# Layer 1's plan: Silu pieces a round later and pinned in ScalarE's order, the attention's exponentials a round later and beside the mixer's

## Chip, cores and metric

One core of a Trainium2 chip. The metric is the device time of one execution in microseconds, the median of the runs shown. In the text PE is TensorE, DVE VectorE, ACT ScalarE, POOL GpSimd, and SP the engine that issues most of the DMAs.

## The reference

A two-layer decoder over 32 sequences of 128 tokens of width 256 in fp32. Layer 0 is an attention with a latent, a cross attention and a mixture of experts (two of eight). Layer 1, which this change is about, has three blocks, each behind a layer norm and added to its input:

```python
x = x + _L1_attn_ref(_layernorm(x, axis=-1), ...)   # gated linear recurrence in chunks of 64, then an MLP with silu
x = x + _L1_xattn_ref(_layernorm(x, axis=-1), ctx_1024, ctx_1024, ...)   # one softmax over 128 keys per token
x = x + _L1_ffn_ref(_layernorm(x, axis=-1), ...)    # quantized linear, convolution of 3 taps, silu, quantized linear
```

In the first block `q` is normalized with a root mean square (here a logarithm and an exponential), the MLP takes `silu(h2 @ fc_w.T) @ proj_w.T`. The second takes `softmax(vis_key @ lang_key.T * scale)`. The third is

```python
h = bit_linear(x, w1)                       # activations rounded to 8 bits by the row's largest value
h = depthwise_conv1d(h.transpose(0, 2, 1), conv_w, conv_b)   # 3 taps along the tokens
h = jax.nn.silu(h.transpose(0, 2, 1))
return bit_linear(h, w2)                    # again rounded by the row's largest value
```

## The kernel before

Layer 0 runs first (attention, then the experts up to about 1150 us). Layer 1 then works in 16 units `u` of two sequences each (`U = 2`, so 256 tokens). A unit goes through four groups of pieces: `d_` (the recurrence), `m_` (the MLP), `e_` (the attention over the context) and `f_` (the quantized block with its convolution). Each piece is a small function in `unit(u)` that issues a few instructions.

The table `PLAN` gives each piece a round, and a new unit starts every `STEP = 11` rounds. So round `t` holds the pieces of several units, each at another stage: a software pipeline in which some seven units are under way at once. Within a round the pieces are issued in the order of the units, older ones first, and then in the plan's order. A scheduler orders the instructions of each engine from this program. `tc.keep_in_program_order(i)` pins instruction `i` behind all that was traced before it on its engine; TensorE's matmuls and transposes (helpers `mm`, L207, and `turned`, L210) and the DMAs of `fetch` are all pinned in this way. The engines run their own streams in order and wait for each other by semaphores.

The pieces that the text speaks of, in the order in which a unit meets them:

- `fetched` issues two DMAs of `yr` on SP (`fetch`, L719); `added` (L1163) adds them to `x` on VectorE, which begins the unit's way.
- `d_stats`, `d_nb`, `d_norm` (L1093), `d_scaled` (L1100), `d_flip` (copy L1112): statistics on VectorE, the root `rs_d` on GpSimd (L1082), `nb_d` on VectorE (L1088), two passes on ScalarE, transposes on TensorE and the copy `hT_d`. `d_q`, `d_a`, `d_k`, `d_g`, `d_v` are the products with `hT_d`. `al_d` (L1201, L1202) and the scans (L1239, L1245) are on VectorE.
- `d_q2` takes `Ln` on ScalarE (L1219), `d_rms` takes `Exp` (L1222) and multiplies on GpSimd (`qn_d`, L1223). `d_state` and `d_gate` follow on VectorE (L1248, L1252, L1254), with a subtraction on GpSimd (L1249) between.
- `m_fc` applies Silu on ScalarE to four products (`sT_m`, L1280). `m_stats` takes the statistics of `x1`, with `rs_m` on GpSimd, and adds `x1` to `x` there (L1269). `hn_m` is `m_scaled` (L1100).
- `e_stats` loads `kv_e` from DRAM on SP (L1298, two buffers, so that a load waits for the `lv_e` of the unit two before). `e_s` makes the scores, and their largest value `nm_e` (L1334). `e_exp` takes two exponentials of 128x128 on ScalarE (L1339), `e_soft` (L1345, L1347) normalizes them into `at_e`, `e_at` transposes them and makes `lv_e` (L1360); `vv_e` is L1321, and `x<-x,y_e` L1366.
- `f_h(k)`, for four pieces `k` of two hidden chunks: product and scaling `d_f` on VectorE (L1399). `f_z(k)`: the middle tap on ScalarE (L1404). `f_taps(k)`: a tap on VectorE for each of the two chunks (L1414), one on ScalarE (`e_f`, L1418, two buffers), and their sum on GpSimd (L1420). `f_silu(k)`: Silu in place on ScalarE (L1427). `f_top(k)`: the largest value over half of the chunks on VectorE (L1433, joined in L1438). `f_am`, `f_rows` (copy `rows2`, L1147) and `f_round(k)` (L1454, L1455) quantize. `f_out` adds the last product to `x` (L1468, `x<-o_f`) and stores it.

ScalarE keeps one table of functions at a time; where the next function is not in it, the built program has a table load (ACT_TABLE_LOAD, under the line of the function that needs it).

Of the kernel before, what the change touches and what calls it, by code (L numbers as in the profile page):

```python
# [13 lines left out]
AF = mybir.ActivationFunctionType  # L14
# [62 lines left out]
def decoder(ctx: ExitStack, tc: tile.TileContext, a: dict, out: bass.AP):  # L77
    nc = tc.nc
    V, A, PE, GP = nc.vector, nc.scalar, nc.tensor, nc.gpsimd
# [919 lines left out]
    def ternary(wf, ones, asum):  # L999
# [19 lines left out]
        (13, "d_v d_q2"), (14, "d_rms d_scan2"), (15, "d_state"), (16, "d_gate"), (18, "m_y"),  # L1019
        (19, "m_stats"), (20, "m_scaled"), (22, "m_flip"), (26, "m_fc0 m_fc1"), (27, "m_fc2 m_fc3"),  # L1020
        (29, "m_out0"), (30, "m_out1 m_out2"), (31, "m_out3"), (32, "e_stats"), (33, "e_nb"),
        (34, "e_norm"), (36, "e_flip"), (39, "e_k e_v"), (45, "e_s"), (47, "e_exp"), (48, "e_soft"),
        (50, "e_at"), (53, "e_y"), (54, "f_stats"), (55, "f_norm"), (56, "f_quant"), (58, "f_flip"),
        (60, "f_h0"), (62, "f_z0 f_h1"), (63, "f_z1 f_h2"), (64, "f_taps0 f_taps1 f_h3"),
        (65, "f_silu0 f_silu1"), (66, "f_z2"), (67, "f_top0 f_z3"), (68, "f_taps2"), (70, "f_silu2"),
        (71, "f_taps3"), (72, "f_silu3"), (73, "f_top1"), (75, "f_am"), (78, "f_rows"),
        (79, "f_round0 f_round1 f_round2"), (81, "f_round3"), (89, "f_out"),
    )

# [5 lines left out]
    def layer1(wd):  # L1035
# [8 lines left out]
        with (  # L1044
# [12 lines left out]
            def sb(tag, name, bufs=1, dt=F32, shape=(2, T)):  # L1057
                of = late if tag in ("z", "d", "kv", "s", "zi") else pool
                return of.tile([P, *shape], dt, tag=tag, name=name, bufs=bufs)
# [7 lines left out]
            def sm(tag, name, w=U, bufs=3):  # L1067
                return small.tile([P, w], F32, tag=f"l_{tag}", name=f"{tag}_{name}", bufs=bufs)
# [81 lines left out]
            def unit(u):  # L1150
# [185 lines left out]
                def e_exp():  # L1336
                    o["at"], o["den"] = sb("at", f"at_{e_}", 2, shape=(U, S)), sm("den", e_)
                    for i in range(U):
                        A.activation(  # L1339
                            o["at"][:, i, :], o["s"][:, i, :], AF.Exp, bias=o["nm"][:, i : i + 1],  # L1340
                            accum_out=o["den"][:, i : i + 1],
                        )

                def e_soft():
                    V.reciprocal(o["den"], o["den"])  # L1345
                    for i in range(U):
                        V.tensor_scalar(o["at"][:, i, :], o["at"][:, i, :], o["den"][:, i : i + 1], None, ALU.mult)  # L1347
# [76 lines left out]

                def f_silu(k):
                    z = o["z"][:, 2 * k : 2 * k + 2, :]
                    A.activation(z, z, AF.Silu)  # L1427

                def f_top(k):

# [43 lines left out]
                for k in range(4):  # L1474
                    for of in (m_fc, m_out, f_h, f_z, f_taps, f_silu, f_top, f_round):
                        pieces[f"{of.__name__}{k}"] = partial(of, k)
# [9 lines left out]
            for u in range(CTX0, NU):  # L1486
                made = context(u, wcs, lambda n: sb("d", n, 4), lambda n: sb("kv", n, 2, shape=(2, U * D)))
                for what, r in zip(("load", "keys", "values"), CTX_ROUNDS[u - CTX0]):
                    between.setdefault(r, []).append(made[what])
            units = [unit(u) for u in range(NU)]  # L1490
            pieces = {r: names.split() for r, names in PLAN}
            for t in range(STEP * (NU - 1) + PLAN[-1][0] + 1):
# [94 lines left out]
def program(arrays):  # L1587
    import concourse.bacc as bacc

    nc = bacc.Bacc("TRN2", target_bir_lowering=False, num_devices=1)  # L1590
    args = {
        k: nc.dram_tensor(f"in_{k}", v.shape, mybir.dt.from_np(v.dtype), kind="ExternalInput").ap()
        for k, v in arrays.items()
    }
    out = nc.dram_tensor("out", arrays["x"].shape, F32, kind="ExternalOutput").ap()
    with tile.TileContext(nc) as tc:
        decoder(tc, args, out)
    return nc
# [9 lines left out]
```

## Time and profile before

| what | value |
|---|---|
| median of 3 runs | 1908.31 us (1905.58 to 1917.17) |
| the profiled execution, its own time | 1910.32 us |
| its span, first to last instruction | 1908.5 us |
| busy over the span: PE, DVE, ACT, POOL | 91%, 59%, 56%, 21% |
| from 1357 to 1685.5 us: PE, DVE, ACT, POOL | 301.25, 282.68, 237.37, 111.49 of 328.50 us |
| layer 1's table loads, each 1283 ns | L1339 29, L1219 16, L1280 16, L1222 3, L1427 3 |
| granted TensorE clock, mean | 0.949 |

Shares over the whole span mix stages with different limits: the experts keep VectorE and ScalarE mostly idle, layer 1 does not. The second row of busy times is eight units of layer 1's steady part, with all groups of pieces under way. In an answer on waits, a line reads "engine, what waited, <- whom it waited for: us in total, times, longest us". In a timeline a line reads "start, duration, engine, line, operation, out<-in, count, and in brackets the idle time just before and what ended it".

### The profile page before, as it was taken

Reading aid. Unit: us, or ns where it says so; the run is one execution under the profiler, and the core shown is the slowest. Engines: PE = TensorE matmul, PEld = TensorE weight load, DVE = VectorE, ACT = ScalarE, POOL = GpSimd, SP = SyncE. Lnnn points to the kernel's source line nnn. Section 1 sums busy time; section 2 is a strip of 40 time slices with the busy share of each in tenths; the row PEclk is TensorE's granted clock in tenths of the full one; section 3 lists DMA queues with packets and bytes.
Section 4 is the critical chain, followed back from the end, with each engine's and each line's share of the span. In section 5 each row is a group of like instructions: output and inputs, shape, how many; then the busy total and the mean of one; then the engine's idle time right before and its main releaser. Section 6 shows DMA issues by size and latency. Waiting matters only on the chain.

```text
span 1908.5 us, 33114 instructions
## 1 busy us (share of the span) xinstructions
PE 1744.7 (91%) x12336; PEld 1427.5 (75%) x12336; DVE 1124.4 (59%) x3767; ACT 1069.7 (56%) x2380; POOL 410.2 (21%) x413
## 2 busy tenths in 40 slices
PE   6999998999888899999999999999899989999853
PEld 3777766776667688888888888788777778778742
DVE  6878775687775613111111104546788888888797
ACT  4565558788884532322232224556777677677662
POOL 4101000000000222222222212222333333333221
PEclk9999998899997799999999999999999999999975
DMA  6000010111001776666676644200000100010000
GB/s 199 2 2 2 13 35 23 34 54 37 24 13 45 254 301 207 243 226 207 216 247 211 215 139 169 72 23 23 23 28 28 50 28 29 29 34 18 28 16 18
DMA packets 58531, 170.12 MB, mean 89 GB/s; under 512 B 6272, under 2 KB 35328, under 8 KB 47616
## 3 DMA queue, kind: packets, MB, share of 16 engines
q1 hardware_dynamic: 51840, 150.14, 23.3%
q0 software_dynamic: 6528, 17.83, 2.4%
q8 instruction: 99, 1.62, 0.4%
q14 instruction: 64, 0.52, 0.1%
HBM read 142.26 MB, written 25.69 MB: 88 GB/s over the span
## 4 chain that ended last, share of the span: by engine, by line
PE 54%; DVE 27%; ACT 8%; POOL 4%; DMA 3%; issue 2%; SPq 0%; POOLq 0%; DVEq 0%; ACTq 0%
PE h L207 12%; PE y L207 12%; ACT sd_b L604 3%; DVE top_f L1433 3%; DMA yr<-ys 3%; DVE z_f L1414 2%; DVE sd_b L594 2%; PE st_a L207 2%; PE et_b L210 2%; PE y_a L207 2%; PE s_a L207 2%; PE od_a L207 2%; PE m_m L207 1%; PE s_b L207 1%; DVE z_f L1454 1%
## 5 line engine op out<-in xcount | busy, mean ns | idle before, releaser
L925 ACT ACTIVATE hTs<-h,moe 128x256 f32<-128x256 f32 (+1 forms) x320 | 140.9, 442 | 334.5 <-PE h L207 324.6
L207 PE MATMUL h<-xTs,moe 128*128 128x256 f32 (+1 forms) x1280 | 243.0, 348 | 1.0 <-DVE xTs L913 1.0
L207 PE MATMUL y<-moe,hTs 128*128 128x256 f32 x1088 | 241.5, 379 | 0.0
L207 PEld LDWEIGHTS h<-xTs,moe 128*128 128x128 f32 x1280 | 214.9, 191 | 24.8 <-DVE xTs L913 1.2
L207 PEld LDWEIGHTS y<-moe,hTs 128*128 128x128 f32 x1088 | 203.8, 190 | 26.0
L604 ACT ACTIVATE sd_b<-sd_b,nan_b 128x128 f32<-128x128 f32 x512 | 153.1, 390 | 29.5 <-DVE nan_b L601 29.5
L913 DVE COPY xTs<-xs 128x512 f32<-128x512 f32 (+1 forms) x40 | 24.4, 610 | 217.7 <-PE xs L210 217.7
L937 DVE TENSOR_TENSOR yt<-y,moe 128x256 f32<-128x256 f32 x68 | 28.8, 424 | 204.7 <-PE y L207 204.7
L594 DVE CUSTOM_DVE_ANT_0 sd_b<-nd_b,s_b 128x128 f32<-128x128 f32 x512 | 112.0, 281 | 21.4 <-PE s_b L207 19.0
L207 PE MATMUL m_m<-wd,sT_m 128*128 128x256 f32 x512 | 119.1, 381 | 0.0
L207 PE MATMUL f_m<-hT_m,wd 128*128 128x256 f32 x512 | 118.9, 388 | 0.0
L1420 POOL TENSOR_TENSOR z_f<-z_f,e_f 128x508 f32<-128x508 f32 x64 | 72.0, 1125 | 211.3 <-DVE z_f L1414 113.2
L938 POOL DMA_INDIRECT ys<-yt,whither x68 | 67.3, 990 | 190.1 <-DVE yt L937 181.9
L207 PEld LDWEIGHTS f_m<-hT_m,wd 128*128 128x128 f32 x512 | 97.7, 195 | 13.4 <-issue 0.5
L899 POOL DMA_INDIRECT xr<-xs,who x68 | 66.0, 970 | 188.8 <-PE xs L210 156.9
L207 PEld LDWEIGHTS m_m<-wd,sT_m 128*128 128x128 f32 x512 | 95.6, 191 | 12.5 <-ACT sT_m L1280 0.2
L145 POOL TENSOR_TENSOR rs_c<-ve_c,mhalf 128x4 f32<-128x4 f32 x8 | 8.1, 1011 | 414.7 <-DVE ve_b L143 286.7
L1427 ACT ACTIVATE z_f<-z_f 128x512 f32<-128x512 f32 x64 | 40.3, 630 | 87.0 <-POOL z_f L1420 86.9
L511 DVE TENSOR_REDUCE nm<-s_a 128x4 f32<-128x512 f32 x128 | 78.8, 676 | 5.1 <-PE s_a L207 4.9
L1404 ACT ACTIVATE z_f<-d_f,pv 128x256 f32<-128x256 f32 x128 | 69.8, 590 | 19.8 <-DVE d_f L1399 19.8
L207 PE MATMUL s_b<-kEO_b,qT_b 32*128 32x256 f32 x512 | 59.7, 453 | 21.1 <-ACT kEO_b L380 17.1
L541 ACT ACTIVATE et_a<-st_a 128x512 f32<-128x512 f32 x128 | 66.4, 613 | 19.0 <-PE st_a L207 19.0
(378 smaller groups left out, 3825.6 us busy)
## 6 DMA issues: line engine op xcount, KB each, us to landing
moe<-in_moe SPq DMA_DIRECT2D x40, 1156.0 KB, 5.9
moe<-in_moe SPq DMA_DIRECT2D x40, 1024.0 KB, 5.2
ckv<-kvc SPq DMA_DIRECT2D x16, 512.0 KB, 3.1
yr<-ys SPq DMA_DIRECT2D x32, 256.0 KB, 3.8
kv_e<-ckv SPq DMA_DIRECT2D x16, 512.0 KB, 3.3
x<-in_x SPq DMA_DIRECT2D x8, 512.0 KB, 9.1
cT_b<-in_ctxT SPq DMA_DIRECT2D x8, 512.0 KB, 3.8
xs<-xn_c SPq DMA_DIRECT2D x8, 512.0 KB, 2.9
```

The source lines that it names most:

```text
L207: tc.keep_in_program_order(PE.matmul(out, lhsT=lhsT, rhs=rhs, start=start, stop=stop))
L511: V.tensor_reduce(nms[i % 2][:, at : at + 2 * (P - HD)].rearrange("p (e x) -> p x e", e=2)[:, :2, :], sp[r], AX.X, ALU.max, negate=True,)
L541: A.activation(et[:, r].rearrange("p j q -> p (j q)"), st[r], AF.Exp)
L594: V.tensor_tensor_reduce(sd[:, r, j, :], nd[:, i, :], sp[r][:, j, :], SLOPES[head(r, j)], -3e38, ALU.add, ALU.max, mx[:, 4 * r + j : 4 * r ...
L604: A.activation(sd[:, r, j, :], sd[:, r, j, :], AF.Exp, bias=nan[:, 4 * r + j : 4 * r + j + 1])
L899: GP.indirect_dma_start(out=xr[h], out_offset=None, in_=xs[:, :], in_offset=bass.IndirectOffsetOnAxis(ap=who[:, q + h : q + h + 1], axis=0),)
L925: A.activation(hT[:, hc, : n * P], p, AF.Relu, bias=b1[:, hc : hc + 1])
L938: GP.indirect_dma_start(out=ys[:, :], out_offset=bass.IndirectOffsetOnAxis(ap=whither[:, q + h : q + h + 1], axis=0), in_=yt[:, h, :], in_ ...
L1404: A.activation(o["z"][:, hc, :], o["d", k][:, j, :], AF.Identity, scale=cw[:, hc, 1:2], bias=cb[:, hc : hc + 1],)
L1420: GP.tensor_tensor(z[:, :, : S - 1], z[:, :, : S - 1], e.rearrange("p h (b t) -> p (h b) t", b=U)[:, :, 1:], ALU.add,)
L1427: A.activation(z, z, AF.Silu)
L1433: V.tensor_reduce(o["top"][:, k, :], o["z"][:, 4 * k : 4 * k + 4, :].rearrange("p h t -> p t h"), AX.X, ALU.max, apply_absolute_value=True,)
```

## The change

The plan is altered in these places: `e_exp` goes from round 47 to 48 and `e_soft` from 48 to 49; `f_silu0` and `f_silu1` go from round 65 to 66, behind `f_z2`; `f_silu2` goes from 70 to 71, behind `f_taps3`; `f_silu3` goes from 72 to 73, `f_top1` from 73 to 74 and `f_am` from 75 to 76. Round 47 of a unit is also round 14 (`d_rms`) of the unit three behind it, which is traced later in that round. The exponentials of `e_exp` and the Silu of `f_silu` are pinned behind what was traced before them on ScalarE. Nothing else is altered. Lines after the edits are two to three further down in the changed kernel (L1404 is L1406 there, L1420 is L1422, L1433 is L1436, L1468 is L1471).

```diff
-        (34, "e_norm"), (36, "e_flip"), (39, "e_k e_v"), (45, "e_s"), (47, "e_exp"), (48, "e_soft"),
+        (34, "e_norm"), (36, "e_flip"), (39, "e_k e_v"), (45, "e_s"), (48, "e_exp"), (49, "e_soft"),
...
-        (65, "f_silu0 f_silu1"), (66, "f_z2"), (67, "f_top0 f_z3"), (68, "f_taps2"), (70, "f_silu2"),
-        (71, "f_taps3"), (72, "f_silu3"), (73, "f_top1"), (75, "f_am"), (78, "f_rows"),
+        (66, "f_z2 f_silu0 f_silu1"), (67, "f_top0 f_z3"), (68, "f_taps2"), (71, "f_taps3 f_silu2"),
+        (73, "f_silu3"), (74, "f_top1"), (76, "f_am"), (78, "f_rows"),
...
                     for i in range(U):
-                        A.activation(
+                        e = A.activation(
                             o["at"][:, i, :], o["s"][:, i, :], AF.Exp, bias=o["nm"][:, i : i + 1],
                             accum_out=o["den"][:, i : i + 1],
                         )
+
+                        tc.keep_in_program_order(e)
...
                     z = o["z"][:, 2 * k : 2 * k + 2, :]
-                    A.activation(z, z, AF.Silu)
+
+                    tc.keep_in_program_order(A.activation(z, z, AF.Silu))
```

## The prediction

> **What bounds the kernel now.** I read the page first, then the busy time by stage, then the waits, then one cycle in order of time. The edit touches only layer 1's plan, so only the part from about 1200 us counts. There one unit of two sequences enters per cycle. The `kv_e` loads start at 1356.90 and again, eight cycles later, at 1685.54: 328.64 / 8 = 41.08 us per cycle.
>
> ```profile
> ACT z_f L1427 <- POOL z_f L1420: 53.0, 32, 4.7
> 1357.00:1685.50 328.50, 301.25 (x1594) 255.38 (x1594) 282.68 (x727) 237.37 (x459) 111.49 (x105) 0.99 0.10 32
> ...
> DVE x L1163 <- DMA yr<-ys: 24.5, 8, 3.8
> DVE pre_d L1252 <- POOL pre_d L1249: 6.3, 8, 0.8
> DVE top_f L1433 <- ACT z_f L1427: 4.5, 7, 1.7
> DVE xn_f L1376 <- POOL rs_f L1082: 2.8, 8, 0.4
> DVE u_d L1244 <- POOL u_d L1213: 2.3, 2, 1.2
> DVE z_f L1414 <- ACT z_f L1404: 1.6, 8, 0.2
> DVE pre_d L1248 <- POOL qn_d L1223: 1.5, 1, 1.5
> ```
>
> These are the waits and the busy time of the eight cycles. The second line gives length, then busy PE, PEld, DVE, ACT, POOL: PE 92%, DVE 86%, ACT 72%. ScalarE's large wait, 53.0 us for GpSimd before the Silu, is idle time of the engine with most room, and so worth nothing by itself. VectorE's waits sum to 43.5 us, 5.4 per cycle; 24.5 of them are the fetch of `yr`, which the edit does not touch. The cycle closes like this:
>
> ```profile
> 1602.73 0.68 DVE L1360 TENSOR_TENSOR lv_e<-lv_e,kv_e 128x512 f32<-128x512 f32 x1
> ...
> 1607.50 0.88 DVE L1163 SCALAR_TENSOR_TENSOR x<-yr,rw,x 128x256 f32<-128x256 f32 x2 [2.85 <-DMA yr<-ys]
> ...
> 1626.37 1.09 POOL L1420 TENSOR_TENSOR z_f<-z_f,e_f 128x508 f32<-128x508 f32 x1 [2.14 <-DVE ms_d L1176]
> ...
> 1626.40 1.07 DVE L1177 TENSOR_TENSOR ms_d<-ms_d,mv_d 128x2 f32<-128x2 f32 x1
> ```
>
> `lv_e` frees the buffer that the `kv_e` load on SP's queue waits for, `yr` is queued behind that load, and VectorE stands at L1163 until it lands (4.1 to 4.4 us from the end of `lv_e`). Then VectorE runs nearly solid until the next `lv_e`. So a cycle is VectorE's work plus its waits, in its own order. The last row shows 0.16 us of work taking 1.07 while GpSimd adds `z_f`; the same happens to L1138 (0.98 us at 1831.22) and L1414 (1.23 at 1844.92), each beside such an add.
>
> ```profile
> 1614.55 0.63 ACT L1427 ACTIVATE z_f<-z_f 128x512 f32<-128x512 f32 x1 [1.20 <-POOL z_f L1420]
> 1615.21 0.51 ACT L1100 ACTIVATE hn_m<-x_m,rs_m 128x256 f32<-128x256 f32 x1
> 1615.63 0.57 ACT L1112 COPY hT_d<-pt_d 128x512 f32<-128x512 f32 x1
> ...
> 1616.24 2.00 PE L207 MATMUL q_d<-hT_d,wd 128*128 128x256 f32 x8 [1.46 <-ACT hT_d L1112]
> ...
> L1339 ACT ACT_TABLE_LOAD x29 | 37.2, 1283 | 0.5
> ```
>
> Here `hT_d` stands behind the Silu pieces on ScalarE, TensorE waits for it, and the attention's exponentials (L1339) cost 29 table loads, two in most units.
>
> **The change, part by part.** The built order of the changed kernel has the same instructions on PE, DVE, POOL and SP, and 13 table loads fewer on ACT (55 against 68): both exponentials now stand behind the mixer's `exp` (L1222) and share its load. TensorE's order within a cycle and SP's queue do not move; nothing is moved past a DMA. What moves is ACT's order, and with it DVE's and POOL's.
>
> *Loads.* 13 x 1.283 = 16.7 us of ACT, counted at nothing: ACT is idle 28% of the cycle, and DVE's waits for what these loads delay (L1248, for `qn_d`) are 1.5 us in eight cycles. Without that cover they would be worth the whole 16.7. The Trainium skill (ScalarE: Activation LUTs, "What ACT_TABLE_LOAD costs") counts a further drain with each switch, 2.66 us in all. The rows do not show it: the load of 1591.28 is followed by its function at 1592.57, 1.29 later. By the page ACT would be spared 34.6 us, still on an engine with room.
>
> I now walk one cycle. Zero is L1163 at 1607.50; the next is at 1648.66, 41.16 later. Durations are those of the same instructions in this cycle.
>
> *Silu behind other work.* The taps' first pass L1404 of piece 2 no longer waits behind Silu 1: it starts when `d_f` is there, 3.66 instead of 3.97. VectorE's taps of piece 2 gain nothing, since GpSimd's add L1269 runs until 4.64 beside them (they began at 1612.09, which is 4.59). `rs_m` follows at 6.2 to 6.9, then `hn_m` twice, `hT_d` at 7.8 instead of 8.1: TensorE gets `hT_d` 0.4 earlier, which nothing on VectorE waits for (`al_d` was ready at 13.1 and taken at 14.59).
>
> *Taps of piece 3.* In the new DVE order the first of them stands right behind `x<-x,y_e` (L1366), before the statistics; it used to come last, at 17.9. It needs ACT's pass of piece 3, which comes after `hT_d` and ends at 9.2. VectorE is free at 7.2: a new wait of 2.0. GpSimd's add of piece 2 starts at about 8.75 and runs 1.1, to 9.85; if it shuts the taps out as in the rows above, the wait is 2.65. Queued behind it: both statistics, `top_f`, `al_d` and the scan, so everything that closes the cycle.
>
> *`rs_d`.* The second statistics of `d` now come just before their use, and on POOL `rs_d` (0.70) is behind the add of piece 3 (1.09), which itself waits for the last taps. VectorE waits from the taps to `nb_d`: 0.09 + 1.10 + 0.70 + 0.03 less 0.17 of own work = 1.75, or about 2.1 if `ve_d` is shut out by that add. This used to be hidden behind the quantization.
>
> *`top_f` of half 1* (1.88) leaves this stretch together with its wait (0.47) and the shut-out of `ms_d` (0.90). From L1163 to `x<-o_f`: 22.53 before; after, 22.53 - 1.88 - 0.47 - 0.90 + 2.03 + 1.75 = 23.06, or with both shut-outs 24.03. So +0.53 to +1.50.
>
> *From `x<-o_f` to the end of `lv_e`:* 14.27 before. `top_f` comes here (+1.85), `rows2` is copied 0.2 late because ACT stands at `xn_d`, which waits for the late `nb_d`; the wait at L1252 goes (-0.87 with its issue) since `at_e` now lies between; `at_e` and the rounding lose some 0.25 less each to GpSimd. Sum 14.95: +0.68.
>
> A cycle is then longer by 1.2 to 2.2 us. I take 2.0, near the upper end, since three rows of the trace show the shut-out. Below these, a bound from the other side: if every VectorE wait but the fetch went, a cycle would shrink by (43.5 - 24.5) / 8 = 2.4.
>
> *Where it ends.* There are nine such cycles (eight, and one more before fetching stops): 9 x 2.0 = 18. Before 1357 TensorE is busy 93% and carries the same work in the same order: 0. In the drain there are two more cycles with the piece 3 wait but fewer stages to hold up: +1, bounds -2 to +5. Sum +19: 1910.3 us + 19 = 1929.3 for an execution like the profiled one (span 1908.5, 1.8 us around it). That execution lies 0.11% above the median of 1908.31, so on the median 1927.3. Its own range is 1916 to 1940.
>
> **The rivals.** *Faster.* ACT was what held the cycle, through the Silu pieces ahead of `hT_d`. For it: 15.2 us of TensorE waits for `hT_d` in eight cycles, and `hT_d` does come earlier. Against it: VectorE never waits for what `q_d` feeds. If it is so, and the new waits prove short, the 2.4 per cycle go: 9 x 2.4 = 21.4, 1887 on the median.
>
> *No net effect.* VectorE's work is the same, and the waits only change places: the moved `top_f` fills what `rs_d` opens, GpSimd's adds come a little later than in my walk. This ends within 3 us of 1908. It is also what follows if the edit does not act, which the built order speaks against.
>
> *Much slower.* `at_e` now stands behind `top_f` on VectorE and falls some 3 us later in the cycle. TensorE does not reach `at_e`'s transposes without it, and behind them in its order are `vv_e` and the product for `d_f` 1, which VectorE takes before L1163. In the walk they end 1.15 us before the fetch lands. If `at_e` is over 1.15 later still, each us beyond that costs 9: two us past it make 1945.
>
> **How the numbers follow.** A measurement of this kernel can tell about 1% from no change (19 us). I give the forecast 0.62: 0.42 of it above 1927.4 and 0.20 below, since its sum sits at that line. Faster 0.12; no effect 0.18; much slower 0.08. So slower by over 1%: 0.42 + 0.08 = 0.50; within: 0.20 + 0.18 = 0.38; faster: 0.12. The range runs from 1895, which cuts off most of the fast case, to 1942.
>
> **What would show it.** ACT table loads 68 to 55. In a cycle: VectorE idle 2 to 2.7 us at the taps of piece 3, put down to ACT's L1406 or hidden in a longer instruction; 1.7 to 2.1 at `nb_d` for POOL's `rs_d`; none at L1252; the `yr` wait near 3 as before; ACT's 53.0 us before the Silu mostly gone with no gain from it; the `kv_e` loads 43 us apart. The forecast is wrong if these loads come 41.1 apart or closer, or if TensorE at `at_e` rather than VectorE sets when L1163 is reached.

## The result, and the profile after

| | before | after |
|---|---|---|
| median, six runs each on one chip | 1908.54 us (1905.25 to 1917.17) | 1928.3 us (1925.4 to 1932.11) |
| ratio after / before, 95% interval | | 1.0109 [1.0083, 1.0135] |
| the profiled execution, its span | 1910.32, 1908.5 us | 1932.11, 1930.3 us |

The change makes the kernel 1.1% slower. To see where, I use one mark per unit, the start of `lv_e` on VectorE; there are 16. Between the third and the twelfth lie the nine cycles that the prediction counts. In the profiled executions:

| stretch | before | after | difference |
|---|---|---|---|
| layer 0 and the first unit, to the first `lv_e` | 1276.06 | 1274.03 | -2.0 |
| filling, first to third `lv_e` | 80.13 | 75.63 | -4.5 |
| nine cycles, third to twelfth | 369.49 (41.05 each) | 388.95 (43.22 each) | +19.5 |
| twelfth `lv_e` to the end | 182.82 | 191.69 | +8.9 |
| span | 1908.5 | 1930.3 | +21.8 |

The first row is no effect of the change: the first `lv_e` came at 1268.15 to 1281.00 in the 14 kernels profiled for this study, which share all of layer 0. A single profile is no better than that there. The span's 21.8 us also compare two single executions, the one after being the longest of its six; between the medians lie 19.8. The cycles are more even, but each kernel's come from one profile: single ones lie between 39.45 and 42.45 us before and between 41.99 and 44.22 after, so some tenths between two kernels can be scatter.

The first block below is the waits and busy times of the changed kernel over its nine cycles ("engine, what waited, <- whom for: us in all, times, longest"; the line of numbers is the window, its length, and busy PE, PEld, DVE, ACT, POOL).

```profile
1349.66:1738.61 388.95, 346.94 (x1801) 293.88 (x1800) 320.89 (x819) 252.59 (x505) 119.52 (x117) 0.97 0.09 31
...
DVE vv_e L1321 <- PE vv_e L207: 25.1, 9, 3.7
DVE nb_d L1088 <- POOL rs_d L1082: 14.1, 9, 1.6
DVE d_f L1401 <- PE h_f L207: 8.9, 9, 1.4
DVE z_f L1416 <- ACT z_f L1406: 5.9, 9, 1.4
DVE x L1163 <- DMA yr<-ys: 3.2, 4, 1.1
...
PE at_e L210 <- DVE at_e L1349: 30.3, 9, 5.4
...
ACT z_f L1406 <- DVE d_f L1401: 40.6, 18, 3.2
ACT xn_d L1093 <- DVE nb_d L1088: 31.5, 9, 3.9
```

VectorE is busy 35.65 us per cycle (320.89 / 9) against 35.43 before; its waits sum to 7.32 against 5.34. So of the 2.17 us by which a cycle grew, 1.98 are new VectorE waits. The list has also changed its members. The fetch of `yr`, 27.3 us in nine cycles before, is down to 3.2; in its place VectorE waits 25.1 for TensorE's `vv_e` and 8.9 for its `h_f`. TensorE waits 30.3 for `at_e` (4.4 before). ScalarE's wait before the Silu is out of its list, and so is TensorE's wait for `hT_d`. Two of these lines in the kernel before, over its nine cycles:

```profile
DVE x L1163 <- DMA yr<-ys: 27.3, 9, 3.8
...
PE at_e L210 <- DVE at_e L1347: 4.4, 6, 0.7
```

Of the table loads, these are left for the attention's and the mixer's exponentials (29 and 3 before):

```profile
L1222 ACT ACT_TABLE_LOAD x16 | 20.5, 1283 | 0.3
L1339 ACT ACT_TABLE_LOAD x3 | 3.8, 1283 | 0.1
```

One cycle of the changed kernel, VectorE in order of time, from one L1163 to the next. The bracket is the idle time before and what ended it:

```profile
1613.17 0.69 DVE L1321 TENSOR_TENSOR vv_e<-vv_e,rv 128x512 f32<-128x512 f32 x1 [3.72 <-PE vv_e L207]
...
1614.38 0.87 DVE L1163 SCALAR_TENSOR_TENSOR x<-yr,rw,x 128x256 f32<-128x256 f32 x2
...
1621.83 0.69 DVE L1401 TENSOR_TENSOR d_f<-h_f,rows_f_sb 128x512 f32<-128x512 f32 x1 [1.36 <-PE h_f L207]
1622.69 0.69 DVE L1368 TENSOR_TENSOR x<-x,y_e 128x512 f32<-128x512 f32 x1 [0.17 <-PE y_e L207]
1623.66 0.92 DVE L1416 SCALAR_TENSOR_TENSOR z_f<-d_f,pv,z_f 128x254 f32<-128x254 f32 x1 [0.28 <-ACT z_f L1406]
...
1637.25 0.16 DVE L1088 SCALAR_TENSOR_TENSOR nb_d<-mv_d,rs_d 128x2 f32<-128x2 f32 x1 [1.65 <-POOL rs_d L1082]
...
1637.79 0.87 DVE L1471 SCALAR_TENSOR_TENSOR x<-o_f,dq_f,x 128x256 f32<-128x256 f32 x2
...
1645.73 1.92 DVE L1436 TENSOR_REDUCE top_f<-z_f 128x256 f32<-128x1024 f32 x1
...
1649.30 1.04 DVE L1349 TENSOR_SCALAR at_e<-at_e,den_e 128x128 f32<-128x128 f32 x2
...
1652.37 0.68 DVE L1362 TENSOR_TENSOR lv_e<-lv_e,kv_e 128x512 f32<-128x512 f32 x1
```

L1163 at 1614.38 has no bracket: its data had long landed, and what held VectorE is `vv_e`. TensorE's side of that is one line:

```profile
1650.29 0.43 PE L210 MATMUL at_e<-cst,at_e 128*128 128x128 f32 x2 [3.12 <-DVE at_e L1349]
```

TensorE stood 3.12 us before `at_e`, which VectorE takes only after `top_f`. In its fixed order `lv_e`, `k_e`, `vv_e` and `h_f` come behind.

These products can also run slower behind such a wait. In the unit before, whose `vv_e` opens the cycle above, TensorE had waited 3.10 us for `at_e`, and from 1607.5 its granted clock is 0.50 for 3.4 us. The same eight matmuls, before and after:

```profile
1599.70 1.89 PE L207 MATMUL k_e<-xT_e,we 128*128 128x256 f32 x8
```

```profile
1608.12 3.28 PE L207 MATMUL k_e<-xT_e,we 128*128 128x256 f32 x8
```

Between the third and the twelfth `lv_e` the clock falls to 0.50 seven times (for 3.4 us, once for 6.8), each time with a wait of at least 3.1 us for `at_e` just before or still under way; in the kernel before it does so twice. The mean granted clock is 0.99 there before and 0.97 after. Two units with the same wait of 3.12 us show no such fall; why, no run here shows. Of the nine units from the third `lv_e` on, six ran `lv_e` and `k_e` wholly or partly at half clock; in five of them VectorE waited 3.2 to 3.7 us for `vv_e` (1.8 in the sixth), in the three at full clock 2.03.

### The profile page after: what moved, and what is told of

The parts are those of the page before. It is cut to its first block, busy times and chain, and to the rows that moved or that the text cites. A ratio compares the mean times of both kernels' runs of the same rounds, so it can differ in the third digit from the quotient of the medians.

```text
span 1930.3 us, 33109 instructions
## 1 busy us (share of the span) xinstructions
PE 1750.3 (91%) x12336; PEld 1430.2 (74%) x12336; DVE 1131.5 (59%) x3767; ACT 1049.0 (54%) x2367; POOL 404.1 (21%) x413
## 4 chain that ended last, share of the span: by engine, by line
PE 57%; DVE 28%; ACT 8%; DMA 2%; POOL 2%; issue 2%; SPq 0%; POOLq 0%; DVEq 0%; ACTq 0%
PE h L207 12%; PE y L207 12%; ACT sd_b L604 3%; DVE top_f L1436 3%; DVE sd_b L594 2%; DVE z_f L1416 2%; PE m_m L207 2%; DVE z_f L1457 2%; PE st_a L207 2%; PE s_a L207 2%; PE od_a L207 2%; PE y_a L207 2%; DMA yr<-ys 2%; PE et_b L210 1%; PE k_e L207 1%
## 5 line engine op out<-in xcount | busy, mean ns | idle before, releaser
L937 DVE TENSOR_TENSOR yt<-y,moe 128x256 f32<-128x256 f32 x68 | 28.9, 425 | 204.6 <-PE y L207 204.6
L1422 POOL TENSOR_TENSOR z_f<-z_f,e_f 128x508 f32<-128x508 f32 x64 | 72.5, 1133 | 271.5 <-DVE z_f L1416 128.7
L1406 ACT ACTIVATE z_f<-d_f,pv 128x256 f32<-128x256 f32 x128 | 69.5, 592 | 59.8 <-DVE d_f L1401 59.4
L1416 DVE SCALAR_TENSOR_TENSOR z_f<-d_f,pv,z_f 128x254 f32<-128x254 f32 x128 | 70.4, 564 | 9.9 <-ACT z_f L1406 9.8
```

The source lines that it names most:

```text
L1406: A.activation(o["z"][:, hc, :], o["d", k][:, j, :], AF.Identity, scale=cw[:, hc, 1:2], bias=cb[:, hc : hc + 1],)
L1416: V.scalar_tensor_tensor(z[:, :, 1:], d[:, j, :].rearrange("p (b t) -> p b t", b=U)[:, :, : S - 1], cw[:, hc, 0:1], z[:, :, 1:], ALU.mult, ...
L1422: GP.tensor_tensor(z[:, :, : S - 1], z[:, :, : S - 1], e.rearrange("p h (b t) -> p (h b) t", b=U)[:, :, 1:], ALU.add,)
```

## The experiments

Theory A is the forecast's: a cycle is VectorE's own order, and the new stalls at piece 3's taps and at `nb_d` make the loss. Theory C is its rival "much slower": the late `at_e` holds TensorE, and through `vv_e` VectorE. Cycles are those between the third and the twelfth `lv_e`; busy and waits are VectorE's per cycle; intervals are at 95%. Each ratio is to the kernel before, measured beside it, whose median lay between 1905.36 and 1910.06 us.

| kernel | us | ratio to before | cycle | busy | waits |
|---|---|---|---|---|---|
| before | 1908.54 | | 41.05 | 35.43 | 5.34 |
| after | 1928.3 | 1.0109 [1.0083, 1.0135] | 43.22 | 35.65 | 7.32 |
| e1_exp | 1916.77 | 1.0059 [1.0037, 1.0081] | 42.19 | 36.57 | 5.36 |
| e2_silu | 1935.74 | 1.0156 [1.0129, 1.0183] | 43.51 | 33.97 | 9.38 |
| e4_plan | 1935.16 | 1.0132 [1.0107, 1.0156] | 43.83 | 35.05 | 8.52 |
| e8_taps3 | 1934.02 | 1.0124 [1.0073, 1.0175] | 43.89 | 35.37 | 8.31 |
| e9_pinadd | 1936.22 | 1.0131 [1.0107, 1.0154] | 43.57 | 36.42 | 6.91 |
| e10_pintaps | 1930.67 | 1.0129 [1.0098, 1.0159] | 42.47 | 36.51 | 5.62 |
| e11_rounds3 | 1907.5 | 0.9990 [0.9966, 1.0015] | 41.02 | 36.47 | 4.27 |
| e6_before_kv | 1894.48 | 0.9914 [0.9892, 0.9936] | 39.78 | 35.92 | 3.61 |
| e5_after_kv | 1942.03 | 1.0163 [1.0141, 1.0186] | 44.75 | 35.06 | 9.49 |
| e12_rounds3_kv | 1928.02 | 1.0099 [1.0071, 1.0128] | 43.31 | 36.51 | 6.52 |
| e13_taps3_kv | 1928.3 | 1.0098 [1.0071, 1.0124] | 43.41 | 36.17 | 7.03 |
| e14_silu_kv | 1927.23 | 1.0092 [1.0064, 1.0121] | 42.34 | 37.66 | 4.52 |

### The halves of the change

**e1_exp**: the exponentials' half alone, plan entry and pin, in the kernel before.

```diff
-(47, "e_exp"), (48, "e_soft")
+(48, "e_exp"), (49, "e_soft")
...
+                        tc.keep_in_program_order(e)
```

> Only the exponentials' part of the edit: e_exp at round 48, e_soft at 49, the exponentials pinned; the Silu pieces as before. VectorE's built order stays that of the kernel before, two loads fewer than there on ACT (66 against 68). Theory A (the VectorE order that came with the f pieces' rounds makes the cycle longer, the exponentials do not): cycle between kv_e loads 40.5 to 41.5 us against 41.1 before and 43.4 after, total 1900 to 1910. Rival B (at_e is late because the exponentials now stand behind the mixer's, and TensorE waits for it): the cycle rises to 42 or more and the total to 1918 or more.

**e2_silu**: the Silu half alone.

```diff
-(65, "f_silu0 f_silu1"), (66, "f_z2"), ... (70, "f_silu2"), (71, "f_taps3"), (72, "f_silu3"), (73, "f_top1"), (75, "f_am")
+(66, "f_z2 f_silu0 f_silu1"), ... (71, "f_taps3 f_silu2"), (73, "f_silu3"), (74, "f_top1"), (76, "f_am")
...
-                    A.activation(z, z, AF.Silu)
+                    tc.keep_in_program_order(A.activation(z, z, AF.Silu))
```

> Only the Silu part: the f pieces' rounds and the pin on Silu; the exponentials as before, 68 loads. VectorE's built order has the taps of piece 3 ahead of the statistics and the last top_f behind the rounding, as in the changed kernel. Theory A: cycle 42.8 to 43.8 us; total 1926 to 1936, since the 6.5 us that the changed kernel gains before 1357 us are lost again if they came from the exponentials. Rival B: cycle near 41.3, total 1905 to 1914.

**e4_plan**: the rounds of both halves without the two pins.

> The rounds of the change without its two pins: 68 table loads again, the Silu pieces back ahead of GpSimd's later pieces on ScalarE, VectorE's order nearly that of the changed kernel (taps of piece 3 ahead of the statistics). Theory A (VectorE's order, that is the new rounds, makes the loss; pins and loads are worth little): cycle 43.0 to 44.5 us, 1925 to 1942 us. Rival P (the pins make it, by holding ScalarE's work in an order that VectorE waits for): cycle 41 to 42 us, 1905 to 1916 us.

e1_exp came out with a cycle of 42.19, nearer its rival: the exponentials' half costs 1.14 us per cycle by itself, which the forecast had at nothing. Its VectorE waits are as long as before (5.36), but they now name `vv_e` (15.2 us in nine cycles) beside the fetch (11.2). VectorE is busy 1.14 longer, since `top_f`'s join and `at_e` fall beside GpSimd's work:

```profile
1634.56 1.42 DVE L1440 TENSOR_TENSOR top_f<-top_f 128x256 f32<-128x256 f32 x1
...
1636.57 1.50 DVE L1349 TENSOR_SCALAR at_e<-at_e,den_e 128x128 f32<-128x128 f32 x2
```

In the kernel of e6_before_kv, 0.40 was enough for the first of them, the same tile and shape.

e2_silu lies where A put it (cycle 43.51), with the wait at piece 3's taps that the forecast foresaw, 2.0 us in each cycle, and that at `nb_d`:

```profile
DVE x L1163 <- DMA yr<-ys: 24.7, 9, 4.0
DVE z_f L1414 <- ACT z_f L1404: 17.7, 9, 2.0
DVE nb_d L1088 <- POOL rs_d L1082: 13.2, 8, 1.6
DVE pre_d L1248 <- POOL qn_d L1223: 11.8, 8, 1.5
```

The halves cost 1.14 and 2.46, together 2.17 in the changed kernel: they do not add up. e4_plan (43.83) shows that the rounds make the loss, +2.78 per cycle, as A expected. By these profiles the pins, with the 13 table loads that they save, give back 0.61 of it; the intervals of the two totals overlap. e4_plan has 68 loads as the kernel before.

### One suspected stall at a time, in the changed kernel

**e8_taps3**: piece 3's taps a round later; with that, `top_f` stands behind `at_e`, and the two stalls stay.

```diff
-(71, "f_taps3 f_silu2"),
+(71, "f_silu2"), (72, "f_taps3"),
```

> The changed kernel with f_taps3 one round later (72). In the built order of VectorE the last top_f now stands behind at_e, all else up to there as in the changed kernel; the early taps of piece 3 and the add ahead of rs_d stay. Theory A (VectorE's own waits at the taps and at nb_d set the cycle; TensorE's wait for at_e mostly takes the place of the fetch): at_e is 1.9 us earlier, the wait for vv_e goes, the yr wait comes back, cycle 0.3 to 1.0 us shorter than 43.4, total 1919 to 1925. Rival C (the late at_e on TensorE sets the cycle): cycle about 2 us shorter, total 1908 to 1913.

**e10_pintaps**: VectorE's taps of piece 3 pinned behind the statistics, which removes both stalls and leaves `at_e` late.

```diff
-                        V.scalar_tensor_tensor(
+                        v = V.scalar_tensor_tensor(
...
+                        if k == 3:
+                            tc.keep_in_program_order(v)
```

> The changed kernel with the VectorE taps of piece 3 pinned behind what was traced before them. In the built order they come after the statistics and ve_d, and on POOL rs_d now precedes the add of piece 3; top_f stays ahead of at_e. So the two VectorE waits of the forecast are taken away, and the late at_e is left. Theory A: the wait at the taps (0.28, and 0.45 of shut-out) and 0.8 of the 1.65 at nb_d go, cycle 41.5 to 42.3 us, total 1908 to 1918. Rival C: TensorE's chain behind at_e still sets when L1163 is reached, cycle 43.0 or more, total 1924 or more.

**e9_pinadd**: GpSimd's add of piece 3 pinned behind `rs_d`.

```diff
-                    GP.tensor_tensor(
+                    g = GP.tensor_tensor(
...
+                    if k == 3:
+                        tc.keep_in_program_order(g)
```

> The changed kernel with GpSimd's add of piece 3 kept behind rs_d, so that nb_d no longer waits for that add; all other orders as in the changed kernel. Theory A (VectorE's stalls add up): the 1.65 us at nb_d go, cycle 41.5 to 42.4 us, 1913 to 1922 us. Theory C (the late at_e decides whatever VectorE gains before it): TensorE waits as long for at_e, cycle 42.9 to 43.4 us, 1926 to 1931 us. In between: the stall is ahead of at_e too, so that at_e comes earlier by it.

None of the three makes the changed kernel faster. In e8_taps3 `at_e` is earlier: TensorE's waits at its transposes fall from 30.3 to 18.8 us in nine cycles (the trace puts 13.1 of these down to ScalarE, but the transposes start as VectorE's `at_e` ends: 1571.73, against 1570.73 + 1.05), and VectorE's wait for `vv_e` falls from 25.1 to 3.1. Yet the cycle is 43.89, above both expectations: the fetch is back at L1163 (22.7), the taps wait 15.6, and a new wait of 12.9 stands at L1248. So C alone does not explain the loss. (Its four runs lie between 1920.72 and 1939.71 us, and the profile is of one of the longest, 1938.76.) In e10_pintaps both stalls are out of the list of waits or nearly so (`nb_d` 1.6 in all, the taps not at all), and `vv_e` is where it was:

```profile
DVE vv_e L1321 <- PE vv_e L207: 24.4, 9, 3.7
DVE d_f L1401 <- PE h_f L207: 7.6, 8, 1.4
...
PE at_e L210 <- DVE at_e L1349: 29.4, 9, 4.5
```

Its cycle is 42.47, between the two expectations and 0.75 less than the changed kernel's, although the waits that went at `nb_d` and at the taps sum to 2.0 per cycle. Part of them came back in another form: `nb_d` itself takes 0.95 us on average instead of 0.16, and a new wait of 0.6 stands at `nb_e` for GpSimd's `rs_e`. So the run does not take the stalls away cleanly, and what they are worth can't be read from it. In the total even the 0.75 is not seen.

e9_pinadd (43.57, just above what C expected) is the clearest case of a wait that changes its form. VectorE first, then GpSimd, in the same cycle:

```profile
1641.55 1.04 DVE L1088 SCALAR_TENSOR_TENSOR nb_d<-mv_d,rs_d 128x2 f32<-128x2 f32 x1 [0.88 <-POOL rs_d L1082]
```

```profile
1640.82 0.70 POOL L1082 TENSOR_TENSOR rs_d<-ve_d,mhalf 128x2 f32<-128x2 f32 x1 [6.36 <-DVE ve_d L1080]
1641.48 1.09 POOL L1422 TENSOR_TENSOR z_f<-z_f,e_f 128x508 f32<-128x508 f32 x1
```

The wait for `rs_d` fell from 1.65 to 0.88, as it should, and `nb_d` itself now takes 1.04 instead of 0.16: it starts 0.07 after GpSimd's add and ends with it. Waits fell by 0.41 per cycle and busy time rose by 0.77.

### The rounds of the second half's end

**e11_rounds3**: the changed kernel with three entries back where they were. Everything else of the change stays: exponentials, pins, 55 table loads, pieces 0 to 2 a round later.

```diff
-(73, "f_silu3"), (74, "f_top1"), (76, "f_am")
+(72, "f_silu3"), (73, "f_top1"), (75, "f_am")
```

> The changed kernel with the ends of a unit's second half back in the rounds of before (Silu of piece 3 at 72, top_f 1 at 73, am_f at 75); the exponentials beside the mixer's, the two pins, the 55 table loads and the later Silu of pieces 0 to 2 stay. VectorE's first half is in the order of before (both statistics ahead of piece 3's taps), and top_f stands behind lv_e, in the fetch's shadow. Theory A (the round's delay of these three pieces makes the stalls at piece 3's taps, at nb_d and at at_e): they go, cycle 40.6 to 41.6 us, 1901 to 1914 us. Rival E (the later exponentials make the loss by themselves, since den_e and at_e come behind pre_d): cycle 42.0 to 42.8 us, 1915 to 1925 us.

Cycle 41.02, ratio 0.9990: the loss is gone, as A said. With the rest of the edit in place, the loss hangs on the one round by which the Silu of piece 3, `top_f` 1 and `am_f` are late; these three were not tried alone in the kernel before. It does not hang on TensorE's clock alone, which falls to 0.50 seven times in these nine cycles as well (mean 0.967, 0.968 in the changed kernel). Nor does the run show that the other parts are free. In the built order of this kernel `top_f` stands between `lv_e` and `vv_e`, where the fetch is on its way; the fetch wait is 1.2 us in nine cycles, against 27.3 before. What remains are other waits:

```profile
DVE z_f L1457 <- ACT rows_f_sb L1147: 10.4, 8, 1.3
DVE vv_e L1321 <- PE vv_e L207: 9.1, 7, 1.4
DVE am_f L1448 <- PE am_f L210: 9.0, 9, 1.1
```

Busy time is 1.04 above the kernel before, waits 1.07 below: a loss and a gain that cancel.

### The fetch

These kernels move the load of `kv_e` on SP's queue behind the fetch of `yr`, so that the fetch no longer waits for the buffer that `lv_e` frees: **e6_before_kv** in the kernel before, **e5_after_kv** in the changed one, **e12_rounds3_kv** in e11_rounds3, **e13_taps3_kv** in e8_taps3. **e14_silu_kv** is e6_before_kv with the Silu pin and pieces 0 to 2 a round later, the rest of the plan as before.

```diff
-                    o["kv"] = sb("kv", f"kv_{e_}", bufs=2, shape=(2, U * D))
-                    nc.sync.dma_start(out=o["kv"], in_=ckv[u])
...
+                def e_kv():
+                    o["kv"] = sb("kv", f"kv_{e_}", bufs=2, shape=(2, U * D))
+                    tc.keep_in_program_order(nc.sync.dma_start(out=o["kv"], in_=ckv[u]))
...
-(34, "e_norm")
+(34, "e_norm e_kv")
```

> The kernel before, with the load of kv_e moved behind the fetch of yr on SP's queue (a piece of its own, at round 34), and VectorE's order then has L1163 ahead of lv_e. Theory A (a cycle of the kernel before is VectorE's work and waits, the fetch wait of 2.8 us in each among them): the wait goes, cycle 38.8 to 39.8 us (TensorE is busy 37.6 in each), 1886 to 1898 us. Rival H (behind the fetch stands another wait of the same length, for TensorE's at_e and what follows it): cycle 40.5 to 41.2 us, 1900 to 1909 us, and the waits of VectorE name vv_e or d_f.

> The changed kernel with the same move of the kv_e load. The waits for piece 3's taps, rs_d and vv_e are untouched. Theory C (in the changed kernel TensorE's chain behind the late at_e has taken the place of the fetch): the fetch is no bound there, cycle 42.6 to 43.4 us, 1922 to 1931 us, with the wait for vv_e or d_f still there. Theory A (the fetch still holds each cycle as before): cycle 40.8 to 42.0 us, 1905 to 1918 us.

> The same kernel, with the load of kv_e behind the fetch of yr as well, so that L1163 stands ahead of at_e and lv_e. Theory A (closers are VectorE's waits, saved loads are worth nothing): as the kernel before with that move, cycle 39.2 to 40.3 us, 1888 to 1900 us. Rival E (at_e, late by the exponentials and now behind L1163 too, holds TensorE): cycle 41.0 to 42.5 us, 1903 to 1920 us.

> The changed kernel with the taps of piece 3 one round later (top_f behind at_e) and the load of kv_e behind the fetch: neither the fetch nor top_f ahead of at_e can close the cycle, the stalls at piece 3's taps (2.0) and at nb_d (1.65) stay. Theory A (the stalls cost what they last once the cycle has no slack): 39.66 of the kernel before with the same move plus up to 3.65, cycle 41.5 to 43.3 us, 1910 to 1930 us. Rival N (they only fill time that the fetch or at_e would have taken, and are free without these): cycle 39.5 to 41.0 us, 1892 to 1908 us.

> The kernel before with the load of kv_e behind the fetch, and the Silu half of the change as far as it leaves VectorE's order alone: the pin, pieces 0 to 2 a round later, piece 3, top_f 1 and am_f in the rounds of before, the exponentials as before (68 table loads). On VectorE at_e stands behind one of the four parts of L1163 and ahead of top_f 1. Theory A (ScalarE's order is off the path, at_e in time): as the kernel before with that move, cycle 39.2 to 40.0 us, 1888 to 1899 us. Rival S (ScalarE's pieces ahead of hT_d were worth something once the fetch is gone): cycle under 39.0 us, under 1886 us. Rival E (the one part of L1163 ahead of at_e already makes TensorE wait): cycle 40.3 to 41.2 us, 1900 to 1910 us.

e6_before_kv is faster than both kernels, as A expected: 1894.48 us, cycle 39.78. Its largest wait on VectorE is now ScalarE's pass, and the fetch waits once, in the first of the nine cycles:

```profile
DVE z_f L1416 <- ACT z_f L1406: 11.9, 17, 1.4
DVE pre_d L1252 <- POOL pre_d L1249: 5.5, 9, 0.8
...
DVE x L1163 <- DMA yr<-ys: 2.9, 1, 2.9
```

So in the kernel before the fetch was a real bound, and its 27.3 us no cover for something else, but 1.27 of the 3.03 us per cycle came back, not all.

The same move in the changed kernel makes it slower, outside both expectations (cycle 44.75). With the fetch early, two of the four parts of L1163 stand ahead of `at_e` in VectorE's order in seven of the nine cycles, and TensorE waits 41.1 us for `at_e` in nine cycles (30.3 in the changed kernel); its mean granted clock there is 0.952. That is C, made worse. (The profile is of the longest of its five runs, 1952.91 us.) e12_rounds3_kv repeats it on the kernel without the three late rounds: all of L1163 stands ahead of `at_e`, TensorE's waits there rise from 19.8 us in nine cycles to 30.9, and the granted clock falls from 0.967 to 0.938. One of these waits:

```profile
1606.45 0.66 PE L210 MATMUL at_e<-cst,at_e 128*128 128x128 f32 x2 [3.79 <-DVE at_e L1351]
```

In e6_before_kv the longest is 0.9: there `at_e`, whose exponentials come a round earlier, is ahead of L1163. That is rival E of e12_rounds3_kv, beyond its numbers. e13_taps3_kv (43.41, at the upper end of A or just above) doesn't decide what it was made for, since L1163 is ahead of `at_e` there too, and TensorE waits 29.5 for VectorE's `at_e`.

e14_silu_kv fell outside all three expectations. `at_e` is in time (TensorE's list doesn't name it), and the cycle is 42.34, 2.56 above e6_before_kv. With the fetch moved, the Silu half costs even with piece 3 in its old rounds: VectorE waits 10.4 us for `rows_f_sb` and 11.3 for the pinned Silu before `top_f`, its busy time is up by 1.74, and TensorE waits more for `hT_d`, which it was to get earlier:

```profile
DVE top_f L1436 <- ACT z_f L1430: 11.3, 9, 1.8
DVE z_f L1457 <- ACT rows_f_sb L1147: 10.4, 8, 1.3
...
PE q_d L207 <- ACT hT_d L1112: 26.7, 9, 4.5
```

## Why the prediction was right, and where it was not

The forecast was 1927.3 us and the measurement 1928.3. By its steps, where the last three rows are of one cycle each, those from 1607.50 before and from 1614.38 after:

| step | forecast | measured |
|---|---|---|
| nine cycles | +18 (2.0 each, bounds 1.2 and 2.2) | +19.5 (2.17 each) |
| before the nine cycles, filling | 0 | -4.5 |
| after them | +1 (-2 to +5) | +8.9 |
| L1163 to `x<-o_f`, 22.53 before | 23.06 to 24.03 | 23.41 |
| from there to the end of `lv_e`, 14.32 before | 14.95 | 15.26 |
| from there to the next L1163, 4.31 before | the same | 4.42 |

Three readings in the prediction are slightly off: its 14.27 is 14.32 by the start and length of `lv_e`; the fetch lands 4.0 to 5.1 us after `lv_e` over the nine cycles, not 4.1 to 4.4; and 7.8 instead of 8.1 makes `hT_d` 0.3 earlier, not 0.4.

**Right.** The cycle, and where it grows. From L1163 to the start of the next `lv_e` the last six cycles take 37.92 to 38.07 us, whether the fetch or `vv_e` had closed the one before; the last six before take 36.16 to 36.70. Over all nine this stretch makes up 1.9 of the 2.17 us. The stall at piece 3's taps is there: 1.36 + 0.17 + 0.28 idle and 0.45 in the lengthened L1416 (0.92 instead of 0.47), 2.26 together where 2.0 to 2.65 were expected; most of it is put down to `h_f`, because TensorE is late as well. Where TensorE is in time, ScalarE's pass alone holds the taps as long: 2.01 in the cycles of e2_silu and e8_taps3. `nb_d` waits 1.65 (1.75 to 2.1 expected). The wait at L1252 is gone; ScalarE's 53 us are gone with no gain; the loads of `kv_e` come 43 us apart. The first part adds up from the forecast's own terms: 22.53 - 1.88 - 0.47 - 0.90 + 2.26 + 1.65 = 23.19; the other 0.2 is a wait at L1259 for TensorE.

**Wrong in the mechanism of the last part.** "The `yr` wait near 3 as before" did not hold. Over nine cycles the part grew a little, from 4.26 to 4.52 on average, but five times in nine L1163 has no fetch wait, and VectorE waits 25.1 for `vv_e` instead. The rival "much slower" had named this chain and given it 1.15 us of slack; the slack was used up, and little more. The five are units in which `lv_e` and `k_e` ran at half clock, with L1163 5.10 to 5.61 us after the start of `lv_e`; in the three at full clock the fetch still lands last, at 4.69 to 5.10. The prediction did not reckon with the clock. The text also held that the forecast would be wrong if TensorE at `at_e` set when L1163 is reached. In these five cycles it does; in the other four the fetch does. So the number has most of its reason from the forecast and a part that it lacked: two loops of nearly the same length close the cycle, and the stalls lie in front of both. That going after one suspect (e8_taps3, e10_pintaps, e9_pinadd) gave back 0.75 us at best, and that the halves of the change do not add, fits this. But none of the three runs took its suspect away without something else in its place, so the price of each single stall stays open.

**The exponentials' half at nothing.** In the walk `at_e` only moved; alone, this half costs 1.14 per cycle (e1_exp).

**The drain, mis-sized.** "Two more cycles with the piece 3 wait but fewer stages to hold up" counted too few. After the twelfth `lv_e` four more follow, and their steps go from 39.3, 32.5, 27.0, 24.8 us to 39.7, 35.0, 29.5, 28.9: +9.5. Between the thirteenth and the last, TensorE's wait for `at_e` goes from 1.5 to 6.3 and VectorE's for the Silu before `top_f` from 0.4 to 4.1. e11_rounds3 gives back 4.0 of the 9.2 us of that stretch; the rest was not taken apart.

**The filling, mis-sized.** "Before 1357 TensorE is busy 93% and carries the same work in the same order: 0" overlooked the first units, two of whose steps became shorter. From the first to the second `lv_e` all nine kernels with the exponentials pinned beside the mixer's take 36.1 us, the five without 37.8 to 37.9. ScalarE has four loads in this step in the kernel before,

```profile
1299.75 1.28 ACT L1339 ACT_TABLE_LOAD   x1
...
1302.00 1.28 ACT L1219 ACT_TABLE_LOAD   x1
...
1304.75 1.28 ACT L1339 ACT_TABLE_LOAD   x1
...
1307.52 1.28 ACT L1280 ACT_TABLE_LOAD   x1
```

and three in e1_exp and in the changed kernel. The first of the four, with its exponential, stands ahead of the copy of `v_d`, behind which VectorE waits 5.6 us (3.8 in the changed kernel, where the copy is ahead of both exponentials). So the order with the shared load is not worth nothing everywhere; how much of the 1.6 us is the load's own 1.28 was not taken apart. In the nine cycles the saved loads bought nothing that can be seen apart from the pins. The other 2.9 us of the filling are in the second step (42.4 to 39.5). Only kernels with both pins show them, and e8_taps3 and e13_taps3_kv, which have both, do not (41.7 and 41.8); their cause stays open.

That filling (-4.5) and drain (+7.9 over the forecast) erred on opposite sides is luck: each by itself is a fifth to two fifths of the whole effect. That forecast and measurement lie within 1 us is luck too: the six runs after scatter over 6.7 us.

## What to carry to other kernels

In a software pipeline that closes through several engines, ask of each wait which other loop is nearly as long; a forecast by one engine's order can get the sum right, but the price of a single stall can't be read off its length: undoing it may bring it back as a longer instruction or as another wait. A plan's round is an ordering instruction to every engine at once: here one round for three small pieces decided 20 us, while the pins and the 13 table loads together gave back 0.61 us per cycle, by one profile each. Where TensorE is made to wait, its granted clock should be read beside the wait. The fill and the drain must be walked as carefully as the steady part: here they made -4.5 and +8.9 us beside the +19.5 of the nine cycles.

## What the runs showed of the hardware

A VectorE instruction of 128x2 elements can take as long as a GpSimd add of 128x508: `nb_d` took 1.04 instead of 0.16 us when it started 0.07 us behind that add, and ended with it (e9_pinadd). Pinning GpSimd's add behind `rs_d` therefore turned a wait into a lengthened instruction, which no list of waits shows; it is seen only in the busy time (+0.77 us per cycle). This is what the Trainium skill states (SBUF — State Buffer, "Who interferes with whom"): a VectorE instruction with two inputs in SBUF and a GpSimd instruction that reads SBUF share a port, and the second to start waits for the whole of the first.

TensorE's granted clock fell to 0.50 for 3.4 us around its waits for `at_e`, and `k_e`'s eight matmuls then took up to 3.28 us instead of 1.89 (changed kernel, unit at 1608.77). So a wait of 3.1 us made the products behind it late by a further 1.7 (VectorE's wait for `vv_e`: 3.72 instead of 2.03). It did not follow every such wait.
